# Layer 1 of a four-layer kernel: planes of z fetched through GpSimd's DMA queue, and x1 loaded into a slot one piece later

## The chip, the cores and the metric

The kernel runs on one core of one Trainium2 chip. The metric is the device time of one execution in microseconds (us); less is better. A core has five engines that run side by side, each with its own order of instructions: TensorE (PE, matmuls; its loads of weights are listed as PEld), VectorE (DVE), ScalarE (ACT), GpSimd (POOL) and SyncE (SP). They wait for one another through semaphores. Transfers between the large memory (HBM) and the on-chip memory (SBUF) are done by 16 DMA engines; an instruction on SyncE, ScalarE or GpSimd only issues a transfer, and the issuing engine's order is the order of issue in its queue.

## The reference, cut to what matters

Four layers are applied to x of 256 x 256 tokens with 128 channels, each as `x = x + layer(groupnorm(x))`. The change lies in the last part of layer 1. That layer is

```python
def _L1_conv_ref(x, Wa1, ba1, Wa2, ba2, Wb1, bb1, Wb2, bb2, ln2_g, ln2_b, Wg, bg, Wz, bz):
    a = sigmoid((x @ Wa1 + ba1) * (x @ Wa2 + ba2))       # 16 channels
    b = sigmoid((x @ Wb1 + bb1) * (x @ Wb2 + bb2))
    g = sigmoid(x @ Wg + bg)                             # 128 channels
    z = einsum('bikc,bkjc->bijc', a, b)                  # 16 products of 256 x 256 matrices
    return g * (_ln(z, ln2_g, ln2_b) @ Wz + bz)

x = x + _L1_conv_ref(_gn(x), ...)                        # x1 -> x2
```

The normalised z (16 channels) is finished and stored in HBM as `znD` before the last part begins. The last part makes the gate g, multiplies the normalised z by Wz, multiplies the two and adds x1. Layer 2 begins with the group norm of the result x2, whose sums are gathered here too.

## The kernel before: the last part of layer 1

x has its 128 channels on the partitions and is handled in 32 pieces (`NSC`) of 2048 tokens (`SC`, 1 MiB each). Thirteen slots (`SLOTS`) hold pieces of x1. The last 13 pieces that the part before needed are still there when this part begins, so it takes those first (`order`), and the other 19 are loaded again from HBM while it runs.

```python
    def load1(s, slot):
        xs[s] = slots[slot].tile([P, SC], F32, name="x1", tag="x1")
        nc.sync.dma_start(xs[s], x1T[:, s * SC : (s + 1) * SC])
    # ... cut ...
            order = [order1[i] for i in (*range(20, NSC), 19, 18, *range(18))]
            by_dve = (5, 11, 17, 23, 29, NSC - 1)

            def fetch_z(i):
                if i < NSC:
                    zs[i] = sb.tile([P, 2, CK], F32, name="p4_z", bufs=2)
                    for m in range(2):
                        nc.sync.dma_start(
                            zs[i][:, m, :],
                            znD.rearrange("k (j b t) -> b j k t", j=8, t=CK)[order[i + 2 * m] % 16],
                        )

            def gate4(i):
                if i < NSC:
                    xt = xs[order[i]]
                    # ... cut: gts[i] is the tile of the gate ...
                    for h in range(2):
                        pg = psg.tile([P, 2, CK], F32, name="p4_pg")
                        for c in range(2):
                            k = 2 * h + c
                            nc.tensor.matmul(
                                pg[:, c, :], lhsT=wgf, rhs=xt[:, k * CK : (k + 1) * CK], start=True, stop=True
                            )
                        nc.scalar.activation(
                            gts[i][:, h * 2 * CK : (h + 1) * 2 * CK], pg.rearrange("p c t -> p (c t)"),
                            AF.Sigmoid, bias=bgf,
                        )

            # ... cut: sum4() squares the last finished piece on ScalarE ...
            LEAD = 4
            fetch_z(0)
            fetch_z(4)
            for i in range(LEAD + 1):
                gate4(i)
            for i, s in enumerate(order):
                xt = xs[s]
                if i > 1 and i % 4 == 1:
                    fetch_z(i + 3)
                half, z = s // 16, zs[i - i % 4]
                pz = [psz.tile([P, 2, CK], F32, name="p4_pz") for _ in range(2)]
                for c in range(4):
                    # ... cut: pz[c // 2] = wz4 x z[:, (i // 2) % 2] ...
                if i:
                    gate4(i + LEAD)
                # ... cut: VectorE multiplies (pz + bz) by the gate, and gathers the sum ...
                if i in by_dve:
                    # ... cut: VectorE adds the product to xt, in two halves ...
                else:
                    nc.gpsimd.tensor_tensor(xt, xt, gt, ALU.add)
                # ... cut: sum4 ...
                if i:
                    s_ = order[i - 1]
                    nc.sync.dma_start(x2T[:, s_ * SC : (s_ + 1) * SC], xs[s_])
                j = i - 3 + SLOTS
                if i > 2 and j < NSC:
                    load1(order[j], (j + 7) % SLOTS)
            sum4()
            nc.sync.dma_start(x2T[:, s * SC : (s + 1) * SC], xt)
```

One fetch of z brings two planes of 256 KB each and serves four pieces: the first plane two of them, the second plane the next two. There are two tiles for z. The gate of piece i+4 is made while piece i is finished, so x1 of piece i+4 is needed then. The new piece is loaded into the slot of piece i-3, and so only after that piece has been stored.

Layer 2 begins with

```python
        def load5(s):
            if s < NSC:
                xs[s] = x5_pool.tile([P, SC], F32, name="p5_x")
                (nc.gpsimd if s < KB else nc.sync).dma_start(xs[s], x2T[:, s * SC : (s + 1) * SC])

        def square5(s):
            if s < NSC:
                sqs[s] = sb.tile([P, SC], F32, name="p5_sq", bufs=4)
                nc.scalar.activation(sqs[s], xs[s], AF.Square, bias=mr2neg, scale=r2)
```

Its tiles lie in memory that the slots of layer 1 held, so they wait for the last stores from there. In the profile, p_z is a tile of z, x a piece of x1, p_g a gate, p_pg and p_pz the products for the gate and with z, p_x and p_sq the tiles of layer 2.

Of the kernel before, what the change touches and what calls it, by code (L numbers as in the profile page):

```python
# [21 lines left out]
NSC = T // SC  # L22
# [10 lines left out]
def kernel(ctx: ExitStack, tc: tile.TileContext, a: dict, out: bass.AP):  # L33
    nc = tc.nc
# [203 lines left out]
    with tc.tile_pool(name="x0", bufs=1) as xres, tc.tile_pool(name="p0", bufs=3) as sb:  # L238
# [170 lines left out]
        with tc.tile_pool(name="p1", bufs=2) as wk_sb, tc.tile_pool(  # L409
# [9 lines left out]
            with tc.manual_schedule():  # L419
# [5 lines left out]
                for i, s in enumerate(order):  # L425
# [25 lines left out]
                    while len(sums) > (i < NSC - 1):  # L451
                        j, sq = sums.pop(0)
# [318 lines left out]
    SLOTS, FIRST = 13, 8  # L771
# [4 lines left out]
# [3 lines that stand above are left out]
# [54 lines left out]
    with x1_scope:  # L833
# [107 lines left out]
        with tc.tile_pool(name="p4", bufs=3) as sb, tc.tile_pool(  # L941
            name="p4psg", bufs=2, space=PSUM
        ) as psg, tc.tile_pool(name="p4psz", bufs=2, space=PSUM) as psz, tc.manual_schedule():
            zs, gts, sums = {}, {}, []
            junk = sb.tile([P, SC], F32, name="p4_junk", bufs=1)
# [5 lines that stand above are left out]
                if i < NSC:  # L951
                    zs[i] = sb.tile([P, 2, CK], F32, name="p4_z", bufs=2)
                    for m in range(2):
                        nc.sync.dma_start(
                            zs[i][:, m, :],
                            znD.rearrange("k (j b t) -> b j k t", j=8, t=CK)[order[i + 2 * m] % 16],
                        )
# [4 lines that stand above are left out]
                    gts[i] = (  # L962
                        gate_pool.tile([P, SC], F32, name="p4_g", tag="g")
                        if i % 7 < 3 else sb.tile([P, SC], F32, name="p4_g", bufs=4)
# [13 lines that stand above are left out]
            def sum4():  # L978
                i = sums.pop(0)
                nc.scalar.activation(  # L980
                    junk, xs[order[i]], AF.Square, bias=c1neg, accum_out=qsum[:, i : i + 1]
# [14 lines that stand above are left out]
                    q = slice(32 * c, 32 * c + 32)  # L996
                    nc.tensor.matmul(
                        pz[c // 2][:, c % 2, :], lhsT=wz4[q, half, :], rhs=z[q, (i // 2) % 2, :],
                        start=True, stop=True,
                    )  # L1000
                if i:
                    gate4(i + LEAD)
                gt = gts.pop(i)
                for h in range(2):
                    hs = slice(h * 2 * CK, (h + 1) * 2 * CK)
                    pzh = pz[h].rearrange("p c t -> p (c t)")
                    nc.vector.scalar_tensor_tensor(
                        pzh if i in by_dve else gt[:, hs], pzh, bz, gt[:, hs], ALU.add, ALU.mult,
                        accum_out=usum[:, 2 * i + h : 2 * i + h + 1],
                    )  # L1010
                if i in by_dve:
                    for h in range(2):
                        hs = slice(h * 2 * CK, (h + 1) * 2 * CK)
                        nc.vector.tensor_tensor(
                            xt[:, hs], pz[h].rearrange("p c t -> p (c t)"), xt[:, hs], ALU.add
                        )
                else:
                    nc.gpsimd.tensor_tensor(xt, xt, gt, ALU.add)  # L1018
                sums.append(i)
                if len(sums) > 1:  # L1020
                    sum4()
                if i:
                    s_ = order[i - 1]
                    nc.sync.dma_start(x2T[:, s_ * SC : (s_ + 1) * SC], xs[s_])
                j = i - 3 + SLOTS
                if i > 2 and j < NSC:
                    load1(order[j], (j + 7) % SLOTS)
            sum4()
            nc.sync.dma_start(x2T[:, s * SC : (s + 1) * SC], xt)
# [50 lines left out]
    with tc.tile_pool(name="x5", bufs=7) as x5_pool, tc.tile_pool(name="p5", bufs=2) as sb, tc.tile_pool(name="p5psX", bufs=1, space=PSUM) as psX, tc.tile_pool(  # L1080
# [90 lines left out]
        for s in range(NSC):  # L1171
            b, j = divmod(s, KB)
# [687 lines left out]
```

## Time and profile before

| | us |
|---|---|
| median of 3 runs | 3412.5 (3410.81 to 3413.81) |
| span of the profiled execution | 3407.4 |
| TensorE busy | 3119.5 (92%) |
| VectorE busy | 2263.4 (66%) |
| ScalarE busy | 2015.3 (59%) |
| GpSimd busy | 1619.7 (48%) |
| last part of layer 1, first product with z to issue of the last store | 1661.9 to 1831.0 |

The share of busy time is a mean over many parts with different limits. The part that the change touches is about 170 us long, one twentieth of the span, and has to be read by itself: by the waits, the chain of waits and the timeline in that stretch of time. A line of the timeline gives start, duration, engine, line of the kernel, operation, what is written and what is read, and in square brackets how long the engine stood idle before it and for what. SPq is SyncE's queue. "<-" in a name reads "written from": `x<-x1T` is the load of x1, `x2T<-x` the store of x2, `p_z<-znD` the fetch of z.

### The profile page before, as it was taken

To read this page: it belongs to the slowest core of one execution; us is meant where nothing else is said; L and a number is where in the kernel's file an instruction comes from. 1 tells how busy PE (TensorE), PEld (TensorE's weight loads), DVE (VectorE), ACT (ScalarE), POOL (GpSimd) and SP (SyncE) were. 2 spreads that over 40 slices of the span, in tenths; PEclk is the share of its full clock that TensorE was granted. 3 is DMA by queue.
4 is the path that set the end of the run, shared out by engine and by line. 5 is a ranking of instruction groups with operands and counts; after the bars stand their busy time and mean duration, and the time that the engine had idled before them with its cause. 6 is when DMAs were issued, how large, how long until landed. Compare 5 with 4: busy or idle time off the path is not lost.

```text
span 3407.4 us, 52669 instructions
## 1 busy us (share of the span) xinstructions
PE 3119.5 (92%) x20266; PEld 1649.2 (48%) x20266; DVE 2263.4 (66%) x2608; ACT 2015.3 (59%) x2204; POOL 1619.7 (48%) x930
## 2 busy tenths in 40 slices
PE   6669999999999999966896999999999999769998
PEld 5415555555555555523332444444999433224444
DVE  5627888888888888843554545444555677748776
ACT  3657777777777777733575544443444466636555
POOL 4146777777777777733463000000555344514434
PEclk7889999999999999978996999999999999979999
DMA  9972333333333333278596667756999899756764
GB/s 396 355 292 84 120 108 119 108 119 111 115 117 109 119 107 119 95 307 312 208 378 277 253 231 290 293 201 261 345 354 349 308 336 335 277 168 202 209 186 131
DMA packets 298235, 750.06 MB, mean 220 GB/s; under 512 B 74954, under 2 KB 145580, under 8 KB 248828
## 3 DMA queue, kind: packets, MB, share of 16 engines
q1 hardware_dynamic: 289371, 734.19, 60.5%
q0 software_dynamic: 8096, 10.86, 0.9%
q8 instruction: 162, 2.65, 0.3%
q10 hardware_dynamic: 512, 1.59, 0.1%
q14 instruction: 94, 0.76, 0.1%
HBM read 458.88 MB, written 287.66 MB: 219 GB/s over the span
## 4 chain that ended last, share of the span: by engine, by line
PE 40%; DMA 5%; DVE 2%; ACT 1%; issue 1%; POOL 1%; SPq 1%; ACTq 0%; POOLq 0%; DVEq 0%
PE p_pm L1152 13%; PE tp_z L1818 7%; PE p_pm L1305 6%; PE p_pm L1540 5%; PE tp_a L1807 2%; PE p_st L1109 1%; PE p_pg L970 1%; PE p_pt L1577 1%; POOL x L1018 1%; PE p_rz L1066 1%; DMA p_z<-znD 1%; DMA p_x<-x3T 1%; DMA p_er<-eD 1%; PE p_rk L1066 1%; PE p_eb L1066 1%
## 5 line engine op out<-in xcount | busy, mean ns | idle before, releaser
L564 DVE TENSOR_TENSOR p_e<-p_S,triT 128x1024 f32<-128x1024 f32 x512 | 609.4, 1212 | 144.5 <-PE p_S L554 144.5
L574 POOL TENSOR_TENSOR p_es<-p_e 128x1024 f32<-128x1024 f32 x256 | 603.8, 2371 | 126.1 <-issue 66.5
L572 ACT ACTIVATE p_e<-p_e,mbT 128x1024 f32<-128x1024 f32 x512 | 552.3, 1139 | 61.3 <-DVE p_e L564 61.2
L1152 PE MATMUL p_pm<-p_zn,wf 128*128 128x512 f32 x1040 | 451.5, 596 | 1.4 <-DVE p_zn L1169 1.4
L539 PE MATMUL p_mm<-p_xn,w 128*128 128x512 f32 x768 | 405.2, 611 | 0.3 <-DVE p_v L534 0.3
L1152 PEld LDWEIGHTS p_pm<-p_zn,wf 128*128 128x128 f32 x1040 | 198.0, 191 | 255.7 <-issue 248.9
L554 PE MATMUL p_S<-p_q,p_k 32*128 32x256 f32 x4096 | 295.6, 401 | 3.5 <-DVE p_e L564 3.3
L1554 POOL TENSOR_TENSOR p_q<-p_q,p_pb 128x2024 f32<-128x2024 f32 x32 | 144.2, 4505 | 255.8 <-DVE p_pb L1548 241.3
L554 PEld LDWEIGHTS p_S<-p_q,p_k 32*128 32x128 f32 x4096 | 186.1, 184 | 159.5 <-PE p_mm L530 91.7
L1818 PE MATMUL tp_z<-p_B,tp_at 128*128 128x256 f32 x1024 | 250.4, 388 | 1.2 <-DMA p_B<-bD 1.0
L513 POOL TENSOR_TENSOR p_xn<-p_xn,p_rs 128x1024 f32<-128x1024 f32 x63 | 151.3, 2402 | 205.4 <-ACT p_xn L508 108.8
L587 PE MATMUL p_o<-p_e,p_v 128*32 128x256 f32 x4096 | 248.5, 383 | 0.0
L1218 POOL DMA_DIRECT2D rs__17959<-rs2D x4 | 2.0, 504 | 512.8 <-DVE p_zn L1145 512.8
L1261 POOL TENSOR_TENSOR k<-k,p_sq 128x512 f32<-128x512 f32 x128 | 163.2, 1275 | 157.1 <-ACT p_sq L1259 157.1
L1371 POOL TENSOR_TENSOR p_x<-p_x,p_g 128x2048 f32<-128x2048 f32 x30 | 136.4, 4547 | 160.2 <-DVE p_g L1358 101.8
L1818 PEld LDWEIGHTS tp_z<-p_B,tp_at 128*128 128x128 f32 x1024 | 185.1, 191 | 23.9 <-DVE tp_at L1809 2.0
L539 PEld LDWEIGHTS p_mm<-p_xn,w 128*128 128x128 f32 x768 | 126.0, 190 | 104.4 <-issue 88.7
L587 PEld LDWEIGHTS p_o<-p_e,p_v 128*32 128x32 f32 x4096 | 120.2, 110 | 110.2 <-ACT p_g L545 41.5
L1260 DVE TENSOR_TENSOR k<-tp_z,k 128x512 f32<-128x512 f32 x128 | 88.6, 692 | 127.1 <-ACT p_sq L1259 127.1
L1257 ACT COPY p_K<-tp_z 128x512 f32<-128x512 f32 x128 | 75.0, 586 | 158.1 <-PE tp_z L1818 158.1
L545 ACT ACTIVATE p_g<-p_mm,bgh 128x512 f32<-128x512 f32 x128 | 88.0, 687 | 131.3 <-PE p_mm L539 131.3
L1185 DVE SCALAR_TENSOR_TENSOR p_b<-p_pm,b2w,p_b 128x1024 f32<-128x1024 f32 x64 | 82.2, 1284 | 124.9 <-PE p_pm L1152 110.5
(372 smaller groups left out, 5964.7 us busy)
## 6 DMA issues: line engine op xcount, KB each, us to landing
p_x<-x2T SPq DMA_DIRECT2D x60, 1024.0 KB
x<-x1T SPq DMA_DIRECT2D x51, 1024.0 KB
p_x<-in_x_dram SPq DMA_DIRECT2D x32, 1024.0 KB
p_x<-xT SPq DMA_DIRECT2D x64, 512.0 KB
x2T<-x SPq DMA_DIRECT2D x32, 1024.0 KB
aD<-p_a SPq DMA_DIRECT2D x32, 1024.0 KB
bD<-p_b SPq DMA_DIRECT2D x32, 1024.0 KB
p_A<-aD SPq DMA_DIRECT2D x32, 1024.0 KB
```

The costliest lines, as they stand in the source:

```text
L513: nc.gpsimd.tensor_tensor(xn, xn, groups[g]["rs"], ALU.mult)
L539: nc.tensor.matmul(pm, lhsT=w, rhs=t["xn"][:, cs_], start=True, stop=True)
L554: nc.tensor.matmul(Ss[h // 2][:, h % 2, u, :], lhsT=t["k"][hp, r * N + u * P : r * N + (u + 1) * P], rhs=t["q"][hp, r * N : (r + 1) * N], ...
L564: nc.vector.tensor_tensor(e[:, :, 2 * p : 2 * p + 2, :].rearrange("p u h n -> p h u n"), Ss[p], triT[:, 2 * p : 2 * p + 2, :, :], ALU.add,)
L572: nc.scalar.activation(e[:, u, :, :], e[:, u, :, :], AF.Exp, bias=mbT[:, u, i : i + 1])
L574: nc.gpsimd.tensor_tensor(es, e[:, 0, :, :], e[:, 1, :, :], ALU.add)
L587: nc.tensor.matmul(t["o"][hp, r % 2, :], lhsT=t["v"][:, r * 2 + u, hp], rhs=e[:, u, h, :], start=(u == 0), stop=(u == 1),)
L1152: nc.tensor.matmul(pm[:, c, :], lhsT=wf2[:, i, :], rhs=zns[s][:, k * CK : (k + 1) * CK], start=True, stop=True)
L1261: nc.gpsimd.tensor_tensor(k2, k2, sq, ALU.add)
L1305: nc.tensor.matmul(pm[:, c, :], lhsT=w, rhs=src[:, k * CK : (k + 1) * CK], start=True, stop=True)
L1540: nc.tensor.matmul(pm[:, 2 * c : 2 * c + 2, :], lhsT=w2c, rhs=src[:, r : r + 2, :], start=True, stop=True)
L1818: nc.tensor.matmul(pz[:, t, :], lhsT=at[:, u, t * P : (t + 1) * P], rhs=Bc[:, u, :], start=(u == 0), stop=(u == 1))
```

## The change

The fetches of z for pieces 8, 12, 16, 20, 24 and 28 (two DMAs each) are issued by GpSimd, in place of SyncE; those for pieces 0 and 4 stay. And the load of x1 takes the slot of piece i-4 in place of piece i-3, so that the store which has to be done first was issued one piece earlier; the first load comes at i = 4 in place of i = 3. What is computed doesn't change, nor how many bytes are moved. The change is meant to let z come past the loads and stores of x, and to keep SyncE from standing in front of a slot that is still being stored.

```diff
@@ -951,7 +951,7 @@
                 if i < NSC:
                     zs[i] = sb.tile([P, 2, CK], F32, name="p4_z", bufs=2)
                     for m in range(2):
-                        nc.sync.dma_start(
+                        (nc.gpsimd if i > 4 else nc.sync).dma_start(
                             zs[i][:, m, :],
                             znD.rearrange("k (j b t) -> b j k t", j=8, t=CK)[order[i + 2 * m] % 16],
                         )
@@ -1022,8 +1022,8 @@
                 if i:
                     s_ = order[i - 1]
                     nc.sync.dma_start(x2T[:, s_ * SC : (s_ + 1) * SC], xs[s_])
-                j = i - 3 + SLOTS
-                if i > 2 and j < NSC:
+                j = i - 4 + SLOTS
+                if i > 3 and j < NSC:
                     load1(order[j], (j + 7) % SLOTS)
             sum4()
             nc.sync.dma_start(x2T[:, s * SC : (s + 1) * SC], xt)
```

## The prediction

> **What bounds the kernel now.** The page comes first: TensorE is busy 92% of 3407.4 us, but in slices 20 to 22 of 40 (about 1620 to 1875 us), where the last part of layer 1 runs, its digits are 8, 9, 6 and 6 while DMA reads 7, 8, 5, 9. So I asked for everything by time from 1600 to 1900 us. The part runs over 32 pieces from 1661.92 us (first product with z) to 1830.97 us (last store issued); piece i below is the i-th. Four of the steps of the chain that ended last, in order of time (start, duration, what):
>
> ```profile
> 1704.55 14.44 DMA p_z<-znD
> ...
> 1727.72 14.28 DMA p_z<-znD
> ...
> 1762.66 9.58 DMA x2T<-x
> ...
> 1830.97 15.39 DMA x2T<-x
> ```
>
> The reader is to see that a plane of z of 256 KB takes 14 us from its issue, and that the last store of x2 takes 15.4 us; layer 2's first squares start only after that store, at 1846.54. The timeline of TensorE shows what the late planes do:
>
> ```profile
> 1734.31 1.14 PE L997 MATMUL p_pz<-p_z,wz 32*128 32x512 f32 x8
> 1735.38 3.70 PE L970 MATMUL p_pg<-x,wgf 128*128 128x512 f32 x8
> 1742.14 1.63 PE L997 MATMUL p_pz<-p_z,wz 32*128 32x512 f32 x8 [3.05 <-DMA p_z<-znD]
> 1743.70 4.86 PE L970 MATMUL p_pg<-x,wgf 128*128 128x512 f32 x8
> 1748.49 1.14 PE L997 MATMUL p_pz<-p_z,wz 32*128 32x512 f32 x8
> ...
> 1767.48 2.09 PE L997 MATMUL p_pz<-p_z,wz 32*128 32x512 f32 x8 [3.39 <-DMA p_z<-znD]
> ...
> 1792.26 1.25 PE L997 MATMUL p_pz<-p_z,wz 32*128 32x512 f32 x8 [3.04 <-DMA p_z<-znD]
> ```
>
> A piece takes 4.70 us undisturbed (1729.61 to 1734.31). Pieces 16, 20 and 24, the first of their fours, wait about 3 us for z, and the matmuls after the wait are slower (4.86 us for eight instead of 3.70). Next the waits of SyncE's queue and the table by stretches (busy us with counts for PE, PEld, DVE, ACT, POOL, then clock, DMA share, GB/s):
>
> ```profile
> SPq L778 <- DMA x2T<-x: 48.9, 11, 8.0
> ```
> ```profile
> 1670.00:1680.00 10.00, 10.00 (x37) 3.76 (x40) 4.99 (x8) 8.35 (x9) 10.00 (x4) 1.00 0.50 211
> 1680.00:1790.00 110.00, 102.01 (x320) 37.32 (x316) 58.58 (x88) 83.16 (x81) 76.23 (x17) 0.95 1.00 381
> 1790.00:1830.00 40.00, 30.54 (x96) 10.71 (x96) 24.01 (x37) 25.37 (x26) 28.98 (x10) 0.80 0.71 285
> 1830.00:1850.00 20.00, 4.90 (x22) 2.19 (x26) 3.51 (x16) 8.96 (x8) 0.25 (x1) 0.50 1.01 417
> ```
>
> The first line: SyncE stands 48.9 us in front of loads of x1, because the slot is still being stored; the z loads behind it in the same queue are issued late. The table: the DMA engines are full from 1680 to 1790, have 29% of 40 us free after that, and are full again until 1850. So there are two limits on top of one another: TensorE waits for z, and the transfers are near saturation as a whole.
>
> **What the Trainium skill says.** "DMA: Bandwidth & Descriptors", section "Issuing engines are not separate DMA queues": issuing from another engine gives no more bandwidth, all queues run on the same 16 engines. The trace agrees: with GpSimd and SyncE both issuing from 1500 to 1570 us, the share is 1.02 and the rate 418 GB/s. Section "Queues, rings and completion order" of the same page: each engine takes turns between the queues that have work, packet by packet. So a small transfer on a queue of its own doesn't stand behind megabytes of another. In that same saturated stretch the stores of layer 1 to abD from GpSimd landed in a median of 5.5 us, which agrees:
>
> ```profile
> abD<-p_ab POOLq DMA_DIRECT2D x46, 64.0 KB, 5.5
> ```
>
> "TensorE: Matmul & The Clock Gate", section "What's actually happening": the clock falls when the engine has been idle. The same table asked in steps of 10 us gives 0.83 from 1740, 1760, 1770 and 1790 on, at and after the z waits, and 1.00 in all other steps from 1670 to 1810.
>
> **The change, part by part.** (1) Twelve DMAs of z (pieces 8, 12, ... 28, two planes each) leave SyncE and go to GpSimd. In GpSimd's order in the changed program they stand behind the addition of piece i-1, i = 5, 9, ... 25. An issue costs GpSimd 0.50 to 0.57 us (range of its DMA instructions for abD and for layer 2), so 12 x 0.55 = 6.6 us in all, 1.1 us per four pieces. An addition takes 4.54 us, 26 of them: 118 us of 165, so this hides. SyncE saves 12 issues of about 0.61 us, which matter to nobody.
>
> When does z arrive? An addition starts about 3.9 us after its piece's first product and ends 4.5 us later, so the issue is at T(i-1) + 8.4 = T(i) + 3.7. A plane is four times an abD store, and takes turns with 8 KB rows of x; I put the first plane at 6 to 8 us and so at T(i) + 12 at worst. It is needed at T(i+3) = T(i) + 14.1. All of the three waits should go, with 2 to 4 us to spare.
>
> Worth on TensorE, from the starts of the first product of each piece: before piece 16, 7.83 - 4.70 = 3.13, after it 6.35 - 4.70 = 1.65; piece 20, 3.46 + 2.86; piece 24, 3.12 + 1.81, less 1.4 that the VectorE piece 23 costs anyway (pieces 5 and 17: 5.86 + 4.97 - 9.40 = 1.4). Sum 4.8 + 6.3 + 3.5 = 14.6 us: piece 28 could begin at 1798.3 instead of 1812.87.
>
> (2) The load of x1 goes into the slot of piece i-4 instead of i-3. The store that it waits for was issued three pieces earlier (14 us) instead of two (9.4 us), so most of the 48.9 us of SyncE's standing go, but three pairs of load and store are then in flight instead of two. The first load comes one piece later, at about 1684.2 instead of 1679.67, and each has five pieces of time (23.5 us) to land instead of six.
>
> (3) The bytes don't change, and so the transfers set what of the 14.6 us can be kept. In MiB after 1670: 32 stores, 19 loads, 3 of z, 7 loads of layer 2, together 61 = 64.0 MB (the table gives 2.1 + 41.9 + 11.4 + 8.3 = 63.8, so the count is right). Of the time from 1680 to 1850 the engines were busy 110 + 28.4 + 20.2 = 158.6 us for 61.6 MB, 389 GB/s. In the changed kernel they idle half of the time until 1684.2 (3.0 MB done), and then have 61.0 MB left: 61.0 / 0.389 = 157 us, end at 1841 instead of 1850, if they are never idle again. That is 9 us. Is it in the way of TensorE too? The last load of x1 has 22 stores, 19 loads and 2.5 MiB of z in front of it or in it, 43.5 MiB = 45.6 MB; less 3.0 at 381 GB/s that is 112 us, 1796; TensorE wants it at T(27) + 1.1 = 1794.7. So x1 arrives just at or 2 to 4 us behind need in the last pieces: additions end some 11 us earlier than now, and the last stores then queue. Both roads give about the same end: the last store lands some 9 us earlier, at about 1837, and layer 2 starts as much earlier and is otherwise unchanged. 3412.5 - 9 = 3403.5 us.
>
> **Rivals.** All of TensorE's 14.6 us are kept: 3398. For it speaks that the chain names z twice with 14 us and that 11.6 us of DMA time were free from 1790 to 1830; against it the ledger above: those 11.6 us are what is reclaimed, and 2 us of early transfer are given up. Second, x1 takes the place of z: loads come later and with a shorter lead, while TensorE runs faster; if the wait for x1 and the slowed clock eat half of it, the gain is 4 to 5 us, 3408. Third, GpSimd's issue comes too late or its descriptors get poor turns between 8 KB rows: then the planes land at 10 to 12 us, one or two of the waits stay, and additions slip by 1.1 us each fourth piece: 3409 to 3414. Fourth, a wait at the end: GpSimd issues layer 2's first three loads ahead of the addition of piece 30, and they need earlier x2 stores to have landed (now 3.55 us in front of them). With a longer backlog of stores that wait can hold up the addition of piece 30; as long as the transfers are full meanwhile it costs nothing, if not 1 to 3 us.
>
> **Range and chances.** The centre is the ledger's 9 us. A gain of 14.6 plus 1 of noise bounds one side, 3397; a gain of 3 to 4 us the other, 3409; runs of before spread by 3 us. Two per cent would be 68 us, more than a third of the part's whole length; nothing here can move that much either way, so 0.98 for within.
>
> **What would show it right or wrong.** In the changed profile: the TensorE rows for pieces 16, 20 and 24 with no wait for p_z, and spacing 4.7; p_z from GpSimd's queue with a median to landing under 8 us; SyncE's wait for x2T in front of L778 well under 20 us; DMA share near 1.0 through 1790 to 1830; layer 2's first squares at 1836 to 1839. If p_z waits remain, step (1) is wrong; if x<-x1T appears in front of L970 with more than 4 us, step (2) was priced too low; if the share dips again after 1790 and the squares still start near 1846, the ledger was not the limit and something at the end of the part is.

## The result, and the profile after

The changed kernel takes 3386.17 us (median of 4 runs, 3383.81 to 3391.3) beside 3411.65 us for the kernel before (4 runs, 3403.84 to 3413.81): a ratio of 0.9931, 95% interval 0.9912 to 0.9951, which is 25.5 us. Two later comparisons with more runs gave 0.9942 (0.9929 to 0.9955; 18.3 us) and 0.9946 (0.9933 to 0.9959; 19.4 us). So the change is worth 18 to 25 us; 9 were predicted, and 3386.17 lies below the range of 3397 to 3409.

The timeline of TensorE of the changed kernel, pieces 16 to 18 (start, duration, engine, line, operation, and in brackets the idle time before it and its cause):

```profile
1734.41 1.14 PE L997 MATMUL p_pz<-p_z,wz 32*128 32x512 f32 x8
1735.48 3.70 PE L970 MATMUL p_pg<-x,wgf 128*128 128x512 f32 x8
1739.11 1.14 PE L997 MATMUL p_pz<-p_z,wz 32*128 32x512 f32 x8
1740.18 3.70 PE L970 MATMUL p_pg<-x,wgf 128*128 128x512 f32 x8
1744.08 2.30 PE L997 MATMUL p_pz<-p_z,wz 32*128 32x512 f32 x8 [0.20 <-PE p_pg L970]
1746.31 3.70 PE L970 MATMUL p_pg<-x,wgf 128*128 128x512 f32 x8
```

There is no wait for z in the whole part. From the third piece on no eight gate matmuls take longer than 3.70 us (4.86 after a wait before), and the pieces follow one another every 4.70 us (4.97 and 5.86 us around a piece that VectorE adds). The instructions of z's fetch on GpSimd (ns of one issue: min, median, max; first and last start; then the time from issue to landing):

```profile
L954 POOL DMA_DIRECT2D p_z<-znD x12: 592/600/624, 1683.4 to 1782.6; - x12
...
DMA to landing us min/median/max: 8.4/10.3/12.2
```

A plane lands in a median of 10.3 us. The planes that count are the first of each pair, which are needed soonest: on GpSimd they land in 8.4 to 10.3 us. Before, the three that TensorE waited for (issued at 1727.72, 1751.27 and 1776.47) took 14.4, 16.2 and 15.8 us until the product that needed them began. The waits of SyncE's queue in the part (us in total, times, longest):

```profile
SPq L778 <- DMA x2T<-x: 1.6, 2, 1.1
```

SyncE's 48.9 us in front of loads of x1 have gone. The busy table (busy us with counts of PE, PEld, DVE, ACT, POOL, then granted clock, DMA share, GB/s), with one stretch of the kernel before in the first line and three of the changed kernel below it:

```profile
1680.00:1780.00 100.00, 92.80 (x292) 34.08 (x292) 51.76 (x78) 74.36 (x73) 68.25 (x16) 0.95 1.00 383
1680.00:1780.00 100.00, 99.03 (x324) 36.59 (x328) 59.01 (x88) 82.68 (x81) 79.76 (x27) 1.00 1.01 401
1780.00:1813.00 33.00, 24.64 (x80) 8.12 (x72) 22.43 (x34) 22.85 (x22) 28.04 (x12) 0.76 0.97 397
1813.00:1827.00 14.00, 3.63 (x14) 1.74 (x14) 2.28 (x13) 4.25 (x6) 0.00 (x0) 0.50 1.01 397
```

TensorE is busy 99.03 of 100 us at full clock, where it had 92.80 at 0.95. The DMA engines are full nearly to the end (0.97 and more), as predicted, but at 401 GB/s where that stretch had 383 before. Last, two steps of the chain that ended last:

```profile
1774.77 18.03 DMA x2T<-x
...
1812.72 14.09 DMA x2T<-x
```

The last store is issued 18 us earlier than before (1830.97; 3.7 of the 18 lie ahead of the part), lands after 14.09 us instead of 15.39, and the first square of layer 2 follows at 1827.29 instead of 1846.54.

For the comparisons below three marks are read from each trace: the start of the last scaling of z on VectorE (L935; 1645.4 before, 1641.7 after), of the last gate product (L970) and of the first square of layer 2 (L1093). From the first to the second is the **run** of TensorE through the pieces, with the fetch of the first z; from the second to the third the **tail**; both together the **stretch**. The names "last gate product at" and "part" in the expectations count from the first product with z instead.

| kernel | run | tail | stretch | ratio (95% interval) |
|---|---|---|---|---|
| before | 167.0 | 34.1 | 201.1 | |
| before, again | 167.0 | 34.3 | 201.3 | 0.9995 (0.9985 to 1.0004) |
| changed | 151.5 | 34.1 | 185.6 | 0.9931 (0.9912 to 0.9951) |
| changed, second time | 151.6 | 33.7 | 185.3 | 0.9942 (0.9929 to 0.9955) |
| changed, third time | 152.9 | 34.0 | 186.9 | 0.9946 (0.9933 to 0.9959) |
| z on GpSimd alone | 151.6 | 36.3 | 187.9 | 0.9939 (0.9927 to 0.9952) |
| slot alone | 163.1 | 34.1 | 197.2 | 0.9974 (0.9965 to 0.9983) |
| slot alone, again | 164.8 | 34.7 | 199.5 | 0.9978 (0.9967 to 0.9989) |
| z on ScalarE | 159.2 | 32.0 | 191.2 | 0.9973 (0.9959 to 0.9987) |
| z earlier, on SyncE | 156.6 | 37.8 | 194.4 | 0.9966 (0.9952 to 0.9980) |
| changed, no loads of x1 | 150.4 | 35.4 | 185.8 | 0.9952 (0.9936 to 0.9968) |
| the same, again | 151.7 | 34.8 | 186.5 | 0.9963 (0.9951 to 0.9976) |
| changed, last store on ScalarE | 151.6 | 33.1 | 184.7 | 0.9945 (0.9933 to 0.9957) |
| before, no z after the fourth plane | 151.8 | 35.3 | 187.1 | 0.9960 (0.9948 to 0.9971) |

The table says most of it already. The change takes 15.0 us from the run (167.0 to a mean of 152.0) and nothing from the tail. Layer 2, from its first square to the first product of layer 3, is 2.6 us shorter (1164.6 and 1166.8 before; 1162.9, 1163.5 and 1163.0 after); with 2.2 us between the two profiles of before, and 1163.4 to 1165.8 in the other kernels of the table, that these belong to the change is not shown. Together with the 0.3 us of the tail's means that is 17.9 us, against 18.3 and 19.4 timed. Of the larger first difference, 25.3 us between the two profiles, 3.7 lie ahead of the part and 4.2 in layer 3. Both of these vary from execution to execution without order: the last scaling starts between 1645.4 and 1646.2 us before and between 1641.7 and 1651.7 after, and layer 3's products take 370.1 and 374.2 us before, 369.8 to 371.6 after and 368.3 to 379.3 in the other kernels.

### The profile page after: what moved, and what is told of

Its sections match the earlier page's. It is cut to its first block, busy times and chain, and to the rows that moved or that the text cites. A ratio compares the mean times of both kernels' runs of the same rounds, so it can differ in the third digit from the quotient of the medians.

```text
span 3382.1 us, 52698 instructions
## 1 busy us (share of the span) xinstructions
PE 3114.7 (92%) x20266; PEld 1647.6 (49%) x20266; DVE 2263.4 (67%) x2608; ACT 2013.9 (60%) x2204; POOL 1626.4 (48%) x942
## 4 chain that ended last, share of the span: by engine, by line
PE 43%; DMA 4%; DVE 2%; ACT 1%; issue 1%; SPq 0%; POOL 0%; ACTq 0%; DVEq 0%; POOLq 0%
PE p_pm L1152 13%; PE tp_z L1818 7%; PE p_pm L1305 6%; PE p_pm L1540 6%; PE p_pg L970 2%; PE tp_a L1807 2%; PE p_st L1109 2%; PE p_pt L1577 1%; DMA x2T<-x 1%; PE p_rz L1066 1%; DMA p_er<-eD 1%; PE p_eb L1066 1%; PE p_rk L1066 1%; PE p_pz L997 1%; DMA p_x<-x3T 1%; PE p_pp L1433 1%
```

## The experiments

Each time is set beside runs of the kernel before on the same chip. A diff is against the kernel that the sentence ahead of it names.

### The two parts of the change, each alone

First the kernel before, unchanged, to see what the comparison gives for nothing:

> The kernel before, once more, against itself. If the 12 us of the gain that lie outside the last part of layer 1 (6 us ahead of it, 6 us in the layers behind it) are scatter from execution to execution, the ratio is 1.000 within 0.002, and the profile puts the start of that part anywhere between 1655 and 1663 us and layer 3 (first to last product with w2c) anywhere between 370 and 374 us. If they belong to the change, these marks repeat the first profile of before within 1 us: 1661.9 and 374.2.

Measured: 3407.47 us beside 3408.35, ratio 0.9995 (0.9985 to 1.0004). Two equal kernels could thus seem up to some 5 us apart here; 18 us are far outside. Its run and tail agree with the first profile to 0.2 us. Of the two marks, layer 3 moved (370.1 us instead of 374.2), so that it is scatter; the first product with z stayed (1661.6 instead of 1661.9), but it comes at 1655.6, 1662.1 and 1668.8 in the three profiles of the changed kernel, and so it is scatter too.

The fetch of z on GpSimd alone, against the kernel before:

```diff
-                        nc.sync.dma_start(
+                        (nc.gpsimd if i > 4 else nc.sync).dma_start(
```

> z through GpSimd, slots as before (i-3). Theory A, z's own queue is what pays: TensorE has no wait for z over 0.5 us, the part (first product with z to first square of layer 2, 184.6 us before, 171.7 after) takes 171 to 174, and the whole gains as much as the full change, 20 to 26 us. Theory B, the standing of SyncE in front of full slots was the cause and z was only behind it: then z gone from that queue helps TensorE too, but the loads of x1 still stand and arrive late, the part takes 177 to 181 and the whole gains 5 to 12.

Measured: 3387.45 us, 20.9 less than before. The run is 151.6 us, as with the whole change, and no wait for z is left. The waits of SyncE's queue in this kernel:

```profile
SPq L778 <- DMA x2T<-x: 32.7, 10, 5.5
```

SyncE still stands 32.7 us in front of loads of x1, and it costs the run nothing: those loads have more time than they need. The tail of this one profile is 36.3 us, about 2 more than with the whole change; its cause was not looked for.

The slot alone, against the kernel before (twice, since the first gave the time of theory B and the waits of theory A):

```diff
-                j = i - 3 + SLOTS
-                if i > 2 and j < NSC:
+                j = i - 4 + SLOTS
+                if i > 3 and j < NSC:
```

> Slots of piece i-4, z on SyncE as before. Theory A: z still stands behind three pairs of load and store in the same queue, 16 us and more; the waits for z stay at 3 us or grow to 5, the part takes 184 to 190, the whole is the same or up to 5 us slower. Theory B: SyncE stands under 10 us in front of loads, z is issued in time and the waits at pieces 16, 20 and 24 fall under 1 us, the part takes 173 to 178, the whole gains 8 to 20.

> The slot change alone, once more, since its profile was of its slowest execution (3411 where the median was 3398). Theory A: the waits for z stay (10 us in sum), the stretch from the scaling of z to the first square takes 195 to 199 us, and the rest of the 10 us gain is in the clock of TensorE or outside. Theory B, SyncE's standing delayed z: a typical execution has the waits under 5 us in sum and a stretch of 188 to 193.

Measured: 3397.84 us (10.5 less than before) and, on another chip, 3405.98 (7.1 less). The waits of TensorE for z in the second of them:

```profile
PE p_pz L997 <- DMA p_z<-znD: 10.1, 3, 3.8
```

The z waits stay: three of them, 10.1 us, against 9.8 to 10.9 in the two profiles of the kernel before. The waits of SyncE's queue in the same kernel show what became of its standing:

```profile
SPq L1024 <- DMA x2T<-x: 20.3, 10, 2.1
SPq L778 <- DMA x<-x1T: 14.2, 8, 3.8
SPq L778 <- DMA x2T<-x: 7.3, 3, 3.4
```

SyncE's standing did not go, it moved: in front of loads for the store in the slot it fell from 48.9 us to 7.3, but it now waits for older stores and loads ahead of its next issue, 53 us in all for transfers against 51 before. And the z that it asks for lands later: the three first planes that TensorE waited for took 19.6 to 20.9 us from issue to product. The run is 2 to 4 us shorter and the time 7 to 10, more than the run and tail explain (3.9 and 1.6 us of the stretch against 201.1); what the rest of this gain is stays open. What is settled is that it does not add to the other part: z alone gives 20.9 us and both together 18.3 in the same comparison, with intervals that overlap.

The whole change again:

> The changed kernel, once more. Median gain 20 to 26 us if the first measurement holds; if part of it was scatter, 12 to 16 us, which is what the part itself gave in the two profiles. Within the profile the part takes 171 to 173 us in both theories.

Measured: 3390.02 us, 18.3 less than before, between the two ranges expected, with run and tail as in its first profile.

### Is it the queue, the engine, or the bytes?

z on a queue of its own, but ScalarE's, against the changed kernel:

```diff
-                        (nc.gpsimd if i > 4 else nc.sync).dma_start(
+                        (nc.scalar if i > 4 else nc.sync).dma_start(
```

> As the changed kernel, but z on ScalarE's queue in place of GpSimd's: a hardware queue of its own, 2 KB packets. Theory A, any queue apart from that of x will do: no waits for z, from the last scaling of z to the first square of layer 2 (201 us before, 185.5 after) 184 to 188, the whole 16 to 24 us faster than before. Rival, it is GpSimd's packets (4 KB in place of 2 KB) that make the transfers as a whole faster: then this is 4 to 6 us slower than the change, 190 to 192 in that stretch.

Measured: 3403.55 us, 9.5 less than before, about half of the change's gain, and a stretch of 191.2 us, in the range of the theory that expected less. TensorE has no wait for z here either, so z was early enough. The timeline of ScalarE shows where the time went:

```profile
1745.85 2.91 ACTq L954 DMA_DIRECT2D p_z<-znD  x2
1748.86 2.12 ACT L973 ACTIVATE p_g<-p_pg,bgf 128x1024 f32<-128x1024 f32 x2 [5.46 <-DMA x<-x1T]
```

and that of TensorE at the same time:

```profile
1745.16 2.30 PE L997 MATMUL p_pz<-p_z,wz 32*128 32x512 f32 x8 [0.19 <-PE p_pg L970]
1750.03 6.62 PE L970 MATMUL p_pg<-x,wgf 128*128 128x512 f32 x8 [2.56 <-ACT p_g L973]
1756.57 1.14 PE L997 MATMUL p_pz<-p_z,wz 32*128 32x512 f32 x8
```

The issue stands in ScalarE's own order, and the bracket of the activation names what the issue itself waited for: a load of x1, with which z has nothing to do. In this program the transfers issued by SyncE and by ScalarE take turns at the same eight semaphores, and an issue waits until the earlier transfer on its semaphore has landed. Of these two fetches the first was let go at 1745.75, by a store that SyncE had issued at 1729.57, the second at 1748.15, by a load of 1731.69; the two issues themselves took 0.58 us each. GpSimd's fetches have semaphores of their own. The activation of a gate was held back for 5.46 us, TensorE then had no free tile of the two for p_pg, stood still, and its next eight gate matmuls took 6.62 us instead of 3.70. From the product of this piece to that of the next 11.41 us passed instead of the 5.86 of the same place in the changed kernel; a second such delay of 2.5 us on ScalarE follows at 1771 and costs TensorE 1.1. The run is 7.2 us longer than the changed kernel's mean, and these two places are 6.7 of it. ScalarE empties what TensorE needs back at once, GpSimd doesn't. What ScalarE would cost if its issues waited for nothing was not tried; the expectation's rival, the size of the packets, isn't needed to explain the time.

z earlier in SyncE's queue, against the kernel before (one plane at a time, four tiles of one plane, asked for three planes ahead):

```diff
-            def fetch_z(i):
-                if i < NSC:
-                    zs[i] = sb.tile([P, 2, CK], F32, name="p4_z", bufs=2)
...
+            def fetch_z(p):
+                if 2 * p < NSC:
+                    zs[p] = sb.tile([P, CK], F32, name="p4_z", bufs=4)
+                    nc.sync.dma_start(
+                        zs[p], znD.rearrange("k (j b t) -> b j k t", j=8, t=CK)[order[2 * p] % 16]
+                    )
...
-                if i > 1 and i % 4 == 1:
-                    fetch_z(i + 3)
+                if i > 1 and i % 2 == 1:
+                    fetch_z(i // 2 + 3)
...
```

> The kernel before with z on SyncE's queue as before and slots i-3 as before, but each plane fetched by itself five pieces ahead of its first use, in place of both planes three pieces ahead; no memory added. Theory A, only the lateness of z counts: no wait for z over 0.5 us, the stretch from the scaling of z to the first square takes 185 to 189 us instead of 201, the whole gains 12 to 22. Rival, the queue must be another one (SyncE's standing delays z whatever the lead, or the transfers are the limit): waits of 1 us and more remain, the stretch takes 192 or more, the whole gains under 9.

Measured: 3401.24 us, 11.9 less than before; the stretch is 194.4 us. The timeline of TensorE:

```profile
1783.84 2.20 PE L995 MATMUL p_pz<-p_z,wz 32*128 32x512 f32 x8 [3.16 <-DMA p_z<-znD]
...
1796.46 1.14 PE L995 MATMUL p_pz<-p_z,wz 32*128 32x512 f32 x8 [1.49 <-DMA p_z<-znD]
```

and one of the waits of GpSimd:

```profile
POOL p_x L1086 <- DMA x2T<-x: 7.4, 1, 7.4
```

Asking earlier took 10.4 us off the run, but two waits stayed, late in the part: waits and stretch as the rival had them, the gain between the two. The two planes had been asked for 17.9 us before their products began. And the tail grew to 37.8 us: GpSimd stood 7.4 us in front of layer 2's loads, for a store of x2, ahead of the last addition that it has to do. That is the fourth rival of the prediction, seen in this kernel; in the changed one GpSimd stands 2.5 us there.

The changed kernel without its 19 loads of x1 (it leaves out the reading of 19 MiB; the pieces work on what the slot holds, so its output isn't the layer's):

```diff
-                    load1(order[j], (j + 7) % SLOTS)
+                    xs[order[j]] = xs[order[i - 4]]
```

> The changed kernel without the 19 loads of x1 in the last part of layer 1: the pieces after the 13th use what the slot holds, so 19.9 of 64 MB are not moved and the result of those pieces is not the layer's. If the transfers are the limit of the changed kernel, as the ledger of the prediction has it, TensorE runs ahead too: last gate product less than 134 us after the first product with z (137.5 in the changed kernel), and the part falls from 171.5 to 155 or less. If TensorE is the limit up to the last gate, that stays at 137 to 138, and only the landing of the last store gets shorter, from 14 us to 5 to 9: part 162 to 167.

Measured: 3398.08 us, 15.0 less than before. Neither theory's numbers for the part were met: first product to first square took 171.2 us, as in the changed kernel (171.7). So both were timed again:

> The changed kernel a second time, beside the three runs below, so that they are compared on one chip. Expected by both theories: 16 to 25 us below the kernel before; the last gate product ends 137 to 138 us after the first product with z, and the tail from there to layer 2's first square is 33.5 to 34.5 us.

> The changed kernel without its 19 loads of x1 in this part (19 MB of about 61 not moved; the pieces use what their slot holds), a second time. Theory C (TensorE's chain of 32 pieces and then a tail of fixed length set the end; the amount moved sets nothing): within 4 us of the changed kernel of the same call, last gate product at 136 to 138, tail 33.5 to 36. Theory L (the ledger of the prediction: megabytes at a full rate set the end): at least 8 us below the changed kernel, a tail under 28 us.

Measured: 3393.51 us for the changed kernel and 3397.81 without the loads, 4.3 us more, just outside theory C's 4. The changed kernel's last gate product came at 135.8 us and not at 137 to 138; its wait for the first z was longer by as much and more, and the run, which holds both, was 152.9. The table by stretches of the kernel without loads:

```profile
1686.00:1786.00 100.00, 99.03 (x322) 36.43 (x320) 59.01 (x88) 82.66 (x81) 79.76 (x27) 1.00 0.70 247
1786.00:1819.00 33.00, 25.52 (x82) 8.44 (x80) 21.59 (x32) 22.27 (x22) 28.82 (x12) 0.77 0.70 241
1819.00:1835.00 16.00, 3.64 (x14) 1.74 (x14) 3.13 (x16) 5.34 (x7) 0.00 (x0) 0.50 1.01 427
```

and the step of its chain that ends the part:

```profile
1819.60 15.09 DMA x2T<-x
```

The DMA engines are busy 70% instead of full, TensorE's row is the same to the hundredth (99.03 of 100 us), and the last store still takes 15.09 us, in a stretch at share 1.01. So the bytes of the part set neither the run nor the tail: theory C held in the part (run 151.7, tail 34.8), the ledger fell. The time was even a few us longer (ratios 0.9952 and 0.9963, against 0.9931 to 0.9946 for the changed kernel), and the profiles put that into layer 3 (376.0 and 374.4 us for its products, 369.8 to 371.6 in the changed kernel), which varies as much between the other kernels; why was not tried.

The kernel before with the 12 later fetches of z left out (3 MB not moved; the first four planes are used again, so the output isn't the layer's), x1's slots as before:

```diff
-                if i > 1 and i % 4 == 1:
-                    fetch_z(i + 3)
-                half, z = s // 16, zs[i - i % 4]
+                half, z = s // 16, zs[i % 8 - i % 4]
```

> The kernel before without the 12 loads of z from the third pair of pairs on (3 MB not moved; the pieces use the first four planes again), x1's slots as before. Theory A (the waits of TensorE for z, and nothing else about the queues, are what the change takes away): no wait for z, last gate product at 136.5 to 138.5, tail 33.5 to 36.5, time 17 to 23 us below the kernel before. Rival (it matters that GpSimd's queue carries bytes beside SyncE's, for the stores and loads that stay): last gate product at 140 or later, time at most 13 us below the kernel before.

Measured: 3395.84 us, 17.0 less than before, last gate product at 137.5 us, tail 35.3: theory A in all three, the time at the edge of its range. Its stretches:

```profile
1680.00:1780.00 100.00, 99.03 (x322) 36.48 (x321) 59.21 (x90) 82.68 (x81) 73.92 (x18) 1.00 1.01 414
1780.00:1812.00 32.00, 25.84 (x83) 8.59 (x81) 20.10 (x31) 22.08 (x22) 26.80 (x9) 0.79 0.58 223
1812.00:1828.00 16.00, 3.63 (x14) 1.73 (x14) 4.62 (x17) 5.73 (x6) 1.37 (x2) 0.50 1.01 427
```

With no z to wait for, the run is 151.8 us, the changed kernel's, although SyncE alone carries everything. What GpSimd's queue gives is z in time, and no more than that. The last load of x1 is issued at 1764.87 here, the engines then have 42% of 32 us free, and the tail is none the shorter.

### What the tail consists of

The last store issued from ScalarE's queue, ahead of the last sum of squares, against the changed kernel:

```diff
-            sum4()
-            nc.sync.dma_start(x2T[:, s * SC : (s + 1) * SC], xt)
+            nc.scalar.dma_start(x2T[:, s * SC : (s + 1) * SC], xt)
+            sum4()
```

> The changed kernel with one edit: the last store of x2 is issued from ScalarE's queue, where nothing stands in front of it, ahead of the last sum of squares, instead of from SyncE's, behind a store and a load of layer 2. Theory C1 (the tail is as long as the last store stands behind other transfers of its queue): the last store lands within 6 to 10 us of its issue instead of 14.1, the tail falls from 34.1 to 27 to 31, and the time falls by 3 to 7 us below the changed kernel of the same call. Theory C2 (the 16 DMA engines are full of layer 2's loads, and whichever queue the store is in, it lands when they have got through): landing 13 to 15 us, tail 33 to 35, time within 2 us of the changed kernel.

Measured: 3391.9 us beside 3393.51 for the changed kernel, ratios 0.9945 and 0.9946: the same. The timeline of ScalarE:

```profile
1820.49 0.34 ACTq L1028 DMA_DIRECT2D x2T<-x  x1
...
1833.95 6.06 ACT L1093 ACTIVATE p_sq<-p_x,mr2neg,gn_rstd 128x2048 f32<-128x2048 f32 x3 [8.84 <-DMA p_x<-x2T]
```

and the chain, with the time from issue to landing (min, median, max) of layer 2's loads by GpSimd:

```profile
1813.52 20.41 DMA p_x<-x2T
...
DMA to landing us min/median/max: 9.7/18.0/21.1
```

Bracket and chain name a load of layer 2 here, but it can't be what the square waited for: the load issued at 1813.52 is the one of 21.1 us, it landed at 1834.6, and the square began at 1833.95. The name comes from a step of that load's semaphore at 1833.92 that was not yet its last. ScalarE's queue was let go at 1833.39, when the store issued at 1820.49 had landed, after 12.9 us. So the first square still waits for the last store, and from an empty queue the store takes 12.9 us where the three profiles of the changed kernel have 13.6 to 14.9: close to C2's 13 to 15, and not C1's 6 to 10. The tail became 0.6 to 0.9 us shorter than in the changed kernel's second and third profile, as C2 expected. Nor does the tail wait for the group norm: in the changed kernel the norm's last factor is there at 1818.35, the square begins at 1827.29. No version here beats the changed kernel by more than its interval.

## Why the prediction was wrong

**Step (1), z on GpSimd: right in its effect, its landing mis-sized.** All waits for z went, and the 14.6 us that the step worked out for TensorE are what the run lost: 15.0 in the mean, of which 14.1 lie behind the first product with z (150.4 and 151.6 us from there to the last gate product before, 137.5, 137.5 and 135.8 after). With them went the slow clock after each wait: 1.00 in the 100 us of the table, 0.95 before, as "TensorE: Matmul & The Clock Gate", section "What's actually happening", says of an engine that stood idle. A first plane was put at 6 to 8 us and took 8.4 to 10.3, a second one up to 12.2. It didn't matter: GpSimd issues a first plane 10.7 to 11.9 us before the product that needs it (the first at 1683.44 for piece 8 at 1695.37), so 1.4 to 3.3 us were to spare, and the second plane has 9 us more. The prediction's reading that z was issued late is not what the runs show: SyncE had asked 11.4 to 12.8 us before TensorE was ready for z, no later than GpSimd does. What fell is the time to landing, from 14.4 to 16.2 us to 8.4 to 10.3. That agrees with the turn-taking between queues in "DMA: Bandwidth & Descriptors", section "Queues, rings and completion order". The issue took 0.60 us, and 12 of them cost TensorE nothing. (The digits of the page at the prediction's start are read some slices off: from 1618 to 1874 us TensorE has 8, 9, 6 and DMA 5, 9, 6. Nothing rests on them.)

**Step (2), the slot: right for the wait only together with step (1), nothing for the time.** SyncE's wait fell from 48.9 to 1.6 us with the whole change; with the slot alone it only moved (53 us in all). And x1 was never late: no wait for its load is left in the first profile, 0.2 us in the third. The delay of 2 to 4 us that step (3) expected from x1 in the last pieces didn't come. Beside z on its own queue the slot's part can't be told from zero: z alone gives 0.9939, both together 0.9942.

**Step (3) failed: "The bytes don't change, and so the transfers set what of the 14.6 us can be kept."** The full share of 1.00 was taken for a limit. The runs show that it was not one: with 19 MiB less to read the run was 150.4 and 151.7 us, with them 151.5 to 152.9. And the term was mis-sized too: 61.0 MB at 389 GB/s were to take 157 us, but the changed kernel moved 396 GB/s (mean of 1677.9 to 1830 us), which makes 154. So its transfers nearly fill the time that TensorE and the tail take, and the share stays at 0.97 to 1.01 although it is not what the part waits for. The step also ran the account straight through to layer 2. The tail is an account of its own: its stores come out of the last pieces, its loads of layer 2 are issued from 1804.01 on, 10.9 us after the last gate product began, and it took 32 to 38 us in every kernel above whatever had been moved earlier. What the transfers can set is the last 15 us, where share and rate are full (1.01 at 427 GB/s) even without the loads of x1, and no ledger of the 170 us tells that.

Of the 16.5 us between the 9 predicted and the 25.5 of the first comparison, its two profiles put 6.5 into the stretch (15.5 instead of 9), and these are this step's. Another 1.7 lie in layer 2, and 7.9 ahead of the part and in layer 3, where profiles differ by as much without order: that much of the miss is luck. In the later comparisons (18.3 and 19.4) 9 falls as far short of the 15.0 that the run lost. The 1 us for noise at the lower end of the range was too little as well: single runs of the unchanged kernel lie between 3401.22 and 3420.27 us.

**The rival that held** is the first: all of TensorE's 14.6 us are kept, 3398 us. The argument used against it, that the 11.6 us of free DMA time "are what is reclaimed", does not hold. The loads of x1 are over then (the last is issued at 1782.28), and stores come only as fast as pieces are finished. The kernel without later z has the same hole, 42% of 32 us, with no wait for z, and its run is as short: the hole needn't be filled for the gain. 3398 is still 4 to 12 us above the three medians, and 14.6 us are 4 to 11 less than the three gains. Up to 2.6 of that is layer 2, which was predicted as otherwise unchanged; its cause wasn't tried. The rest differs between the three comparisons and is not settled. The third rival (planes at 10 to 12 us, one or two waits stay) was right for the second planes, which have time; the first ones came in 8.4 to 10.3 us, within their lead of 10.7 to 11.9.

Of the signs that the prediction named, no wait for z, spacing of 4.7, SyncE's wait under 20 us and a share near 1.0 through 1790 to 1830 came true; a landing under 8 us and first squares at 1836 to 1839 did not. The squares came at 1827.29. The sign "share near 1.0" could not tell the ledger from its rival, since both allowed it; the kernel without loads could.

The page that the prediction cites for "issuing from another engine gives no more bandwidth" ("DMA: Bandwidth & Descriptors", section "Issuing engines are not separate DMA queues") goes on to say that several issuing engines only save the time of issuing. Here the measurement decides otherwise: with the same engines at the same share, z on GpSimd alone gave 20.9 us, since a small transfer needn't stand behind loads and stores of 1 MiB in SyncE's queue.

## What to carry to other kernels

A saturated share of the DMA engines doesn't say that the bytes set the pace: take out transfers that nobody needs for the question and see whether the end moves, before writing a ledger. If a small, urgent transfer stands behind large ones in one queue, give it a queue whose engine has time, and look whether its issue waits there for the large ones all the same: on ScalarE's queue it did, ahead of an activation that TensorE needed, and half of the gain was lost. And count the tail by itself, from the last product to the first instruction of the next layer: here it kept its length whatever was moved ahead of it.

## What the runs showed of the hardware that was not expected

With z fetched outside SyncE's queue or not at all, the full DMA engines moved more in the same 100 us (1680 to 1780): 383 GB/s before, 401 in the changed kernel, 395 with z on ScalarE, 414 without z, and 369 with z plane by plane on SyncE, at a share of 0.98 to 1.01 in all five. So "full" covers at least 12% of rate; what makes the difference was not tried. And 16 engines at 427 GB/s let one store of 1 MiB take 15.09 us. They move some 6 MiB in that time (427 GB/s times 15.09 us), five of them other transfers, and from an otherwise empty queue such a store still took 12.9 us.
